# A two-layer graph and attention kernel: one load queue, a second expert's products in the first attention's last pairs, rows of the graph layer placed under the experts, and an end of the second attention written out by hand

## The chip, the cores and the metric

The kernel runs on one core of a Trainium2 chip. The metric is the device time of one execution in microseconds. Five engines run their own instruction queues: TensorE (PE, with its weight loads listed apart as PEld), VectorE (DVE), ScalarE (ACT), GpSimd (POOL) and SyncE (SP), which issues nearly all DMA transfers. Matmuls of float32 data appear in the trace as two matmul instructions each, called halves below.

## The reference

N is 1250 nodes with 512 features, 41,250 directed edges. Cut to what matters:

```python
x = x + gnn0(layernorm(x))        # alpha = h@wc ; mean over neighbours of h@wn ; + bias
x = x + ffn0(layernorm(x))        # causal attention, 8 heads of 64, then 8 experts:
    # y = attention(...) @ Wo ; gate = softmax(y @ gate_W + gate_b)
    # hid = gelu(y @ W1[e] + b1[e]) (512 -> 256) ; out = sum_e gate_e * (hid @ W2[e] + b2[e])
x = x + gnn1(layernorm(x))        # h@W_self + mean over neighbours @ W_neigh + bias, layernorm, gamma, beta
x = x + ffn1(layernorm(x))        # depthwise conv of width 3, then attention that keeps the
    # 16 best keys of each query: softmax over those, weighted values, @ wo + wo_b
```

## The kernel before

Rows are cut into T = 10 tiles of P = 125 nodes. `tile_usual` does all the work; at its end it reads one flag, `bad`, and only if that is set runs `tile_general`, which does not happen on these inputs. The stages by the trace: edge counts and the first graph layer up to about 310 us (with the projections of the first attention), the first attention to 620, eight experts to 889, the second graph layer with convolution and projections to 1126, the second attention to 1558.

**Start.** The edge lists `dst_i` and `src_i` (125 rows each) are loaded on SP's queue, and the first node weights `w_n` (1 MB) on ScalarE's queue at the same time; on SP the first part of `X`, `w_c`, and the other four parts of `X` follow. VectorE builds one-hot matrices from the edge lists (`one_hots`), TensorE counts with them (`counts`), and node work (`node_stats` to `node_own`) is put between the rounds.

**First attention.** Its order is written out by hand. A step n is a pair of heads of one row tile, 40 steps in the tile order 7, 9, 8, 6, 5, ..., 0, and two drain steps 40 and 41. Step n makes the scores of n+1, the maxima (`largest0`) and Exp (`weights0`) of n, the transpositions of n−1 (`turns0`), the weighted values of n−2 (`values0`) and one projected quarter (`project0`). The scores of one step in small tiles share one PSUM tile `S` of 1536 columns, of which the last 512 are free. In steps 26, 29, 32 and 35 (`FILL`) TensorE also makes products of expert 0's first weights with row tiles 4 to 9 into those free columns, four matmuls spread over the step; VectorE copies the sum to `parts`, places in the memory of V that are not needed any more.

**Experts.** For each expert e, `hidden` makes the products of `yT` with W1 in three chunks of tiles (0 to 4, 4 to 8, 8 to 10) and two halves f of 128, ScalarE applies Gelu, and `outputs` multiplies with W2, while VectorE adds gate times product to X (L1320). For expert 0 the chunks from tile 4 on are taken from `parts`. Expert weights come in three places of `wpool`, two experts ahead, on SP.

**Second graph layer.** Rows (`bias1`, `gamma`, `beta1`, `v_b`, `wo_b`) and work tiles (`work1`) are opened after the experts have closed their places, and the rows loaded there. For each tile: a norm of X (`stats`, `normed`), transpositions (L859), ScalarE's copy to `inT`, the product with `w_m` (L865). The scheduler, not the hand, orders this part and most of the experts.

**Second attention.** Again by hand, 40 steps (i, j) of a row tile and a head pair. Per step and head: best 8, replaced, next 8 (VectorE), Exp and Sign (ScalarE), product of the two `e·sg` (GpSimd, L1636), transpositions in five groups (`turn1`, `keep1`, one PSUM bank), values of the step n−2, and the sums of the softmax (`sums1`, `sums_exp1`, `sums_over1`, `sums_wide1`, `sums_turn1`, `sums_keep1`, `scale1`). The same loop runs three steps more to drain, with conditions (`final`) for the last tile; `project1` multiplies a tile's result with `w_o`, and `finish1` adds X and stores. After the loop a count of the signs (whether each row kept exactly 16) is summed over the partitions on GpSimd with `partition_all_reduce` (L1822) and gives `bad`.

Of the kernel before, what the change touches and what calls it, by code (L numbers as in the profile page):

```python
# [9 lines left out]
F32 = mybir.dt.float32  # L10
# [10 lines left out]
P = 125  # L21
# [551 lines left out]
def tile_usual(ctx: ExitStack, tc: tile.TileContext, a: dict, out: bass.AP):  # L573
# [24 lines left out]
    def span(t0, t1):  # L598
        return slice(t0 * P, t1 * P)

    def load_w(w, name, queue=nc.sync):
        t = wpool.tile([128, K, D], F32, tag="w", name=name)
        queue.dma_start(t, w.rearrange("(k p) f -> p k f", p=128))
        return t

    def load_expert(e):
# [53 lines left out]
    nc.sync.dma_start(dst_i, a["dst_c"])  # L660
    nc.sync.dma_start(src_i, a["src_c"])

    w_n = load_w(a["wn"], "w_n", nc.scalar)
    for t in range(0, T, 2):
        nc.sync.dma_start(X[:, t : t + 2, :], a["x"].rearrange("(t p) d -> p t d", p=P)[:, t : t + 2, :])
        if t == 0:
            w_c = load_w(a["wc"], "w_c")

    bias0 = row(a["bias0"], "bias0")
# [321 lines left out]
    def on(n):  # L991
        return 0 <= n < len(steps)
# [17 lines left out]


    SMALL = 6 * K
    FILL = {26: (0, 8, 10), 29: (1, 8, 10), 32: (0, 4, 8), 35: (1, 4, 8)}
    ps_s0a_pool = tc.tile_pool(name="ps_s0a", bufs=1, space=PSUM, side="right", reuse_waits="tile")
    ps_s0 = {0: ps_s0a_pool.__enter__()}
    shared = [None]
# [60 lines left out]
    parts = [V_all[:, 4 * D + f * 6 * P : 4 * D + (f + 1) * 6 * P] for f in range(2)]  # L1077

    def part(f, t0, t1):
        return parts[f][:, span(t0 - 4, t1 - 4)]  # L1080

    with tc.tile_pool(name="att0", bufs=2, side="right", reuse_waits="tile") as at0:
# [60 lines left out]
        def fills0(n):  # L1145

            if n not in FILL:
                return []
            f, t0, t1 = FILL[n]
            w1 = experts[0][0]  # L1150
            ps = shared[0][:, 1024 : 1024 + (t1 - t0) * P]

            def fill(k):
                nc.tensor.matmul(ps, w1[:, k, f * 128 : (f + 1) * 128], yT[:, k, span(t0, t1)],
                                 start=(k == 0), stop=(k == K - 1))
                if k == K - 1:
                    nc.vector.tensor_copy(part(f, t0, t1), ps)

            return [lambda k=k: fill(k) for k in range(K)]

# [58 lines left out]
        for n in range(len(steps) + 2):  # L1219
            finish0()  # L1220
            turns = turns0(n - 1)
            fills = fills0(n)

            def turn(last=False):
                for f in turns if last else turns[:1]:
                    f()
                del turns[: len(turns) if last else 1]
                for f in fills if last else fills[:1]:
                    f()
                del fills[: len(fills) if last else 1]  # L1230

            if n > 0:
                largest0(n, 0)
            turn()
            values0(n - 2, 0)
            if n > 0:
                weights0(n, 0)
            largest0(n, 1)
            if len(turns) > 2:
                turn()  # L1240
            values0(n - 2, 1)
            scores0(n + 1, 0)
            weights0(n, 1)
            if len(turns) > 3:
                turn()
            values0(n - 2, 2)
            sums_over0(n)
            scale0(n - 2)
            if len(turns) > 1:
                turn()  # L1250
            scores0(n + 1, 1)
            if len(turns) > 1:
                turn()
            turn(last=True)
# [17 lines left out]
    close(ps_s0a_pool)  # L1272
    psum_pool = tc.tile_pool(name="psum_moe", bufs=3, space=PSUM, reuse_waits="tile")
    psum = psum_o = psum_pool.__enter__()


    with tc.tile_pool(name="moe", bufs=2, side="right") as moe:
# [45 lines left out]
        for e in range(E):  # L1323
# [8 lines left out]
            late = CHUNKS[1:] + CHUNKS[:1] if e == 0 else CHUNKS  # L1332
            for f in range(FF // 128):
                for t0, t1 in late:
                    if e == 0 and t0 > 0:
                        nc.scalar.activation(hid[:, f, span(t0, t1)], part(f, t0, t1),
                                             AF.Gelu_apprx_tanh, bias=b1[:, f : f + 1])
                        continue
                    hidden(e, hid, w1, f, t0, t1)
            if e == 0:  # L1340
# [12 lines left out]
    rows1_pool, rows1 = pool("rows1", 1)  # L1353
    bias1 = row(a["bias1"], "bias1", pool=rows1)
    gamma = row(a["gamma"], "gamma", pool=rows1)
    beta1 = row(a["beta"], "beta1", pool=rows1)
    v_b = row(a["v_b"], "v_b", pool=rows1)
    wo_b = row(a["wo_b"], "wo_b", pool=rows1)
    slots_pool, slots = pool("slots", 1)
    work_pool, work = pool("work1", 2)  # L1360
# [146 lines left out]
    normed1(T - 1)  # L1507
    project1_(0, 2, w_k, 0)
    turn1_(T - 1)
    close(work_pool)  # L1510
    project1_(0, 2, w_k, 1, 2, 3)
    values1_(0, 2)
    for f in range(K):
# [13 lines left out]
    close(slots_pool, rows1_pool, wpool_pool, rows_pool)  # L1527
    psum_pool.__exit__(None, None, None)


# [11 lines left out]
    with (  # L1542
# [86 lines left out]
        def select1(n, a_):  # L1629
            if not 0 <= n <= last:  # L1630
                return
            sg = at1.tile([P, N], F16, tag=f"sg{a_}", name="sg", bufs=1)
            nc.scalar.activation(sg, score.pop((n, a_))[:, :N], AF.Sign, bias=found.pop((n, a_)),  # L1633
                                 accum_out=signs[:, 2 * n + a_ : 2 * n + a_ + 1])
            e = es[n, a_]
            nc.gpsimd.tensor_mul(e, e, sg)  # L1636

        def turn1(n, g):
            if not 0 <= n <= last:
# [74 lines left out]
        def project1(i, c, width=D // K):  # L1714

            y = ps_o1.tile([128, 512], F32, tag="o", name="O")[:P, :width]
            cols = slice(c * width, (c + 1) * width)
            for k in range(K):
                nc.tensor.matmul(y, oTs[i][:, k, :], w_o[:, k, cols], start=(k == 0), stop=(k == K - 1))  # L1719
# [17 lines left out]
        def keep_late1():  # L1737
            if lates:
                t, ps = lates.pop(0)
                nc.vector.tensor_add(V[:, t, :], ps[:P], v_b)  # L1740

        stacks, sums, oTs, ys, projected, lates = {}, {}, {}, {}, [], []
        with tc.manual_schedule():
            nc.sync.dma_start(w_v, a["qkv"][:, 2 * D :].rearrange("(k p) f -> p k f", p=128))
# [1 line left out]
            for a_ in range(2):  # L1746
                halves1(0, a_)
            scores1(0, 0, 2, 0, 1)
            for n in range(len(steps) + 3):


                i, c = n // K - 1, n % K
                i = i if i < T else None
                final = i == T - 1
                if i is not None and i >= 0 and c == 1 and not final:
                    sums_over1(i)
                first1(n, 0)
                values1(n - 2, 0, 5)
# [15 lines left out]
                keep1(n - 1, 1)  # L1774
                second1(n, 0)
                outputs1(n - 2)
                if i is not None and i >= 0:
                    if c == 0:
                        sums1(i)
                    if c == 1 and not final:  # L1780
                        sums_wide1(i)
                    if c == (1 if final else 2):
                        sums_turn1(i)
                        sums_keep1(i)
                    if c == (1 if final else 3):
# [4 lines left out]
                if final:  # L1790
                    project1(*((i - 1, c, D // 2) if c < 2 else (i, 0, D)))
                elif i is not None and i >= 1:
                    project1(i - 1, c)
                scores1(n + 1, 0, 2)
                keep1(n - 1, 2)
                if i is not None and i >= 0 and c == 0:
                    sums_exp1(i)
                    if final:
                        sums_over1(i)
                        sums_wide1(i)  # L1800
                if n == 0:
                    keep_late1()
                without1(n, 1)
# [10 lines left out]
                    keep_late1()  # L1814
                finish1()

        nc.vector.tensor_scalar(signs, signs, float(N - 2 * TOPK), None, op0=ALU.add)
        nc.vector.tensor_mul(signs, signs, signs)
        worst = at1.tile([P, 2], F32, name="worst", bufs=1)
        nc.vector.tensor_reduce(worst[:, 0:1], signs, AX.X, ALU.add)  # L1820
        nc.vector.tensor_copy(worst[:, 1:2], edges)
        nc.gpsimd.partition_all_reduce(worst, worst, P, bass_isa.ReduceOp.add)  # L1822
        missing = at1.tile([1, 1], F32, name="missing", bufs=1)
        nc.vector.tensor_scalar(missing, worst[0:1, 1:2], -1.0, float(NE), op0=ALU.mult, op1=ALU.add)
        nc.vector.tensor_tensor(missing, missing, worst[0:1, 0:1], ALU.max)
        nc.vector.tensor_scalar(bad, missing, 0.5, None, op0=ALU.is_gt)
# [62 lines left out]
```

## Time and profile before

| what | us |
|---|---|
| median of 3 runs | 1566.55 (1565.73 to 1567.2) |
| the profiled execution | 1567.34 |
| its span in the profile | 1565.5 |
| busy: TensorE | 1448.4 (93%) |
| busy: VectorE | 891.0 (57%) |
| busy: ScalarE | 708.6 (45%) |
| busy: GpSimd | 441.5 (28%) |

The profile is of one execution; its own time stands 1.8 us above its span. A timeline row has the start in us, the duration in us, engine, line of the kernel, operation, output and inputs, and in brackets how long the engine stood idle before it and what ended that. A window row has the stretch, its length, the busy time of each engine with the number of instructions, the granted clock of TensorE, the share of the DMA engines and GB/s.

### The profile page before, as it was taken

Reading aid. Unit: us, or ns where it says so; the run is one execution under the profiler, and the core shown is the slowest. Engines: PE = TensorE matmul, PEld = TensorE weight load, DVE = VectorE, ACT = ScalarE, POOL = GpSimd, SP = SyncE. Lnnn points to the kernel's source line nnn. Section 1 sums busy time; section 2 is a strip of 40 time slices with the busy share of each in tenths; the row PEclk is TensorE's granted clock in tenths of the full one; section 3 lists DMA queues with packets and bytes.
Section 4 is the critical chain, followed back from the end, with each engine's and each line's share of the span. In section 5 each row is a group of like instructions: output and inputs, shape, how many; then the busy total and the mean of one; then the engine's idle time right before and its main releaser. Section 6 shows DMA issues by size and latency. Waiting matters only on the chain. (4 is left out here: it accounts for less than half of the span.)

```text
span 1565.5 us, 21452 instructions
## 1 busy us (share of the span) xinstructions
PE 1448.4 (93%) x8133; PEld 949.0 (61%) x8133; DVE 891.0 (57%) x1395; ACT 708.6 (45%) x1352; POOL 441.5 (28%) x634
## 2 busy tenths in 40 slices
PE   5999999979999998999999899989898999999995
PEld 3556744457777766454444446654466777777773
DVE  7895667544444332412222434654498999999892
ACT  2334434455555543110001123331278888888882
POOL 1010000011111220000000032240177888888882
PEclk9999999989999997999999999999999999999998
DMA  4001000010101010000001100000200000000000
GB/s 146 18 0 54 1 1 0 7 44 14 41 18 48 22 26 31 27 27 27 27 27 54 47 22 19 2 26 0 80 11 11 17 19 21 21 21 21 21 8 23
DMA packets 42323, 41.12 MB, mean 26 GB/s; under 512 B 25738, under 2 KB 30084, under 8 KB 42211
## 3 DMA queue, kind: packets, MB, share of 16 engines
q1 hardware_dynamic: 41683, 38.61, 8.2%
q8 instruction: 66, 1.08, 0.3%
q10 hardware_dynamic: 528, 1.05, 0.2%
q14 instruction: 46, 0.38, 0.1%
HBM read 26.81 MB, written 2.56 MB: 19 GB/s over the span
## 5 line engine op out<-in xcount | busy, mean ns | idle before, releaser
L1636 POOL TENSOR_TENSOR e<-e,sg 125x1250 f32<-125x1250 f32 x80 | 206.1, 2577 | 36.2 <-ACT sg L1633 32.6
L1320 DVE SCALAR_TENSOR_TENSOR X<-ps_o,gate,X 125x512 f32<-125x512 f32 x80 | 60.1, 751 | 192.5 <-PE ps_o L1318 192.5
L1584 PE MATMUL S<-K,stacks 128*125 128x512 f32 (+1 forms) x480 | 124.4, 383 | 27.2 <-ACT sg L1633 23.9
L1646 PE MATMUL ps_t<-ident,e 125*125 125x125 f32 x800 | 133.8, 290 | 12.3 <-ACT R L1687 6.0
L1318 PE MATMUL ps_o<-we,hid 128*125 128x512 f32 x320 | 141.0, 595 | 0.0
L1653 ACT ACTIVATE pT<-ps_t 125x500 f32<-125x500 f32 x200 | 118.0, 590 | 49.0 <-PE ps_t L1646 48.0
L1598 DVE MAX8 best<-S 125x8 f32<-125x1250 f32 x80 | 117.0, 1462 | 36.5 <-PE S L1584 35.6
L1646 PEld LDWEIGHTS ps_t<-ident,e 125*125 125x125 f32 x800 | 106.8, 189 | 47.8 <-ACT pT L1653 27.8
L1310 PE MATMUL ps_mm<-yT,we 128*128 128x500 f32 (+1 forms) x352 | 125.9, 516 | 0.0
L1313 ACT ACTIVATE hid<-ps_mm,b 128x500 f32<-128x500 f32 (+1 forms) x44 | 26.9, 612 | 218.5 <-PE ps_mm L1310 218.5
L1618 DVE MAX8 best<-rest 125x8 f32<-125x1250 f32 x80 | 117.1, 1464 | 2.7
L1609 DVE MATCH_REPLACE8 rest<-best,S 125x1250 f32<-125x1250 f32 x80 | 116.0, 1450 | 0.0
L1702 PE MATMUL O<-pT,yT 125*64 125x125 f32 x1600 | 112.8, 279 | 0.0
L1633 ACT ACTIVATE sg<-S,below 125x1250 f16<-125x1250 f32 x80 | 104.8, 1310 | 16.4 <-POOL below L1619 16.3
L1626 ACT ACTIVATE e<-S,nm 125x1250 f32<-125x1250 f32 x80 | 104.2, 1302 | 2.7 <-DVE rest L1609 1.6
L1584 PEld LDWEIGHTS S<-K,stacks 128*125 128x125 f32 x480 | 75.4, 190 | 48.7 <-ACT sg L1633 30.3
L1318 PEld LDWEIGHTS ps_o<-we,hid 128*125 128x125 f32 x320 | 59.2, 187 | 71.6 <-issue 71.3
L1310 PEld LDWEIGHTS ps_mm<-yT,we 128*128 128x128 f32 x352 | 66.3, 189 | 59.6 <-issue 57.5
L1374 POOL TENSOR_TENSOR X<-X,beta 125x512 f32<-125x512 f32 x10 | 12.8, 1305 | 309.1 <-DMA beta<-in_beta 298.8
L1005 POOL TENSOR_TENSOR stacks<-yT,stacks 64x125 fp32r<-64x125 f32 x80 | 34.3, 428 | 232.2 <-ACT stacks L1004 228.8
L1126 ACT COPY pT<-ps_t 125x500 f32<-125x500 f32 (+3 forms) x112 | 54.8, 489 | 94.9 <-PE ps_t L1121 93.9
L1702 PEld LDWEIGHTS O<-pT,yT 125*64 125x64 f32 x1600 | 84.9, 137 | 14.2 <-issue 0.4
(230 smaller groups left out, 2668.6 us busy)
## 6 DMA issues: line engine op xcount, KB each, us to landing
we<-in_W SPq DMA_DIRECT2D x16, 512.0 KB
stacks<-stacks SPq DMA_DIRECT2D x160, 31.2 KB
stacks<-stacks SPq DMA_DIRECT2D x40, 125.0 KB
X<-in_x SPq DMA_DIRECT2D x5, 500.0 KB
out<-y SPq DMA_DIRECT2D x10, 250.0 KB
w_n<-in_wn ACTq DMA_DIRECT2D x1, 1024.0 KB
w_c<-in_wc SPq DMA_DIRECT2D x1, 1024.0 KB
w_q<-in_Wq SPq DMA_DIRECT2D x1, 1024.0 KB
```

What stands on the lines that cost most here:

```text
L1310: nc.tensor.matmul(ps[:, :n], w1[:, k, f * 128 : (f + 1) * 128], yT[:, k, span(t0, t1)], start=(k == 0), stop=(k == K - 1))
L1318: nc.tensor.matmul(ps[:P], hid[:, f, span(t, t + 1)], w2[:, f, :], start=(f == 0), stop=(f == FF // 128 - 1))
L1584: nc.tensor.matmul(score[n, a_][:, n0:n1], stacks[i][:, x, h, :], K2[:, h, n0:n1], start=(x == 0), stop=(x == 1))
L1598: nc.vector.max(out=top[:, 0:8], in_=score[n, a_][:, :N])
L1609: nc.vector.match_replace(out=rest, in_to_replace=top[:, 0:8], in_values=score[n, a_][:, :N], imm_value=LOWEST)
L1618: nc.vector.max(out=top[:, 8:16], in_=rest)
L1626: nc.scalar.activation(e, score[n, a_][:, :N], AF.Exp, bias=found[n, a_][0])
L1633: nc.scalar.activation(sg, score.pop((n, a_))[:, :N], AF.Sign, bias=found.pop((n, a_)), accum_out=signs[:, 2 * n + a_ : 2 * n + a_ + 1])
L1636: nc.gpsimd.tensor_mul(e, e, sg)
L1646: nc.tensor.transpose(turned[n, g][:P, span(b - g0, b - g0 + 1)], es[n, b // T][:, span(b % T, b % T + 1)], ident[:P, :P])
L1653: nc.scalar.activation(pTs[n][:, g0:g1, :], turned.pop((n, g))[:P, : (g1 - g0) * P].rearrange("p (t n) -> p t n", n=P), AF.Relu)
L1702: nc.tensor.matmul(outs[n][a_ * DH : (a_ + 1) * DH, :P], V[:, t, h * DH : (h + 1) * DH], pT[:, a_ * T + t, :], start=(t == 0), stop=(t == ...
```

## The change

- `w_n` is loaded on SP's queue like the others, behind the edge lists and the first part of X.
- `FILL` gets four more entries: expert 1's products for tiles 4 to 9, in steps 37, 38 and in the drain steps 40 and 41 (which take a PSUM tile of their own). From step 37 on two of the four matmuls of a fill have places of their own. Expert 1 takes its chunks from tile 4 on from `parts`, and V's pool is closed after expert 1 instead of after expert 0.
- The pools of the graph layer's rows and work tiles are opened, and the rows loaded, before the experts' pool; `gate` and `stacks` stay open to the end of the layer.
- The loop of the second attention runs over the 40 steps alone, and what followed is written out: all of tile 8's projection in one PSUM tile, the last sums earlier, tile 9's projection one term at a time. The last `e·sg` goes to VectorE. The check sums go through a matmul with ones instead of GpSimd's reduction.

```diff
-    w_n = load_w(a["wn"], "w_n", nc.scalar)
     for t in range(0, T, 2):
         nc.sync.dma_start(X[:, t : t + 2, :], ...)
         if t == 0:
+            w_n = load_w(a["wn"], "w_n")
             w_c = load_w(a["wc"], "w_c")
...
-    FILL = {26: (0, 8, 10), 29: (1, 8, 10), 32: (0, 4, 8), 35: (1, 4, 8)}
+    FILL = {26: (0, 0, 8, 10), 29: (0, 1, 8, 10), 32: (0, 0, 4, 8), 35: (0, 1, 4, 8),
+            37: (1, 0, 8, 10), 38: (1, 0, 4, 8), 40: (1, 1, 8, 10), 41: (1, 1, 4, 8)}
...
-            f, t0, t1 = FILL[n]
-            w1 = experts[0][0]
+            e, f, t0, t1 = FILL[n]
+            w1 = experts[e][0]
+            if not on(n):
+                shared[0] = ps_s0[n % 2].tile([128, 3 * 512], F32, name="S")
             ps = shared[0][:, 1024 : 1024 + (t1 - t0) * P]
...
             values0(n - 2, 0)
+            for f in fills[:1] if n > 36 else ():
+                fills.pop(0)()
             if n > 0:
                 weights0(n, 0)
...
             if len(turns) > 3:
                 turn()
+            for f in fills[:1] if n > 36 else ():
+                fills.pop(0)()
             values0(n - 2, 2)
...
+    rows1_pool, rows1 = pool("rows1", 1)
+    bias1 = row(a["bias1"], "bias1", pool=rows1)
+    gamma = row(a["gamma"], "gamma", pool=rows1)
+    beta1 = row(a["beta"], "beta1", pool=rows1)
+    v_b = row(a["v_b"], "v_b", pool=rows1)
+    wo_b = row(a["wo_b"], "wo_b", pool=rows1)
+    work_pool, work = pool("work1", 2)
     with tc.tile_pool(name="moe", bufs=2, side="right") as moe:
...
-                    if e == 0 and t0 > 0:
+                    if e < 2 and t0 > 0:
-                        nc.scalar.activation(hid[:, f, span(t0, t1)], part(f, t0, t1), ...
+                        nc.scalar.activation(hid[:, f, span(t0, t1)], part(e, f, t0, t1), ...
...
+            if e == 1:
                 close(qkv0_pool)
-    close(gate_pool, stacks_pool)
...
-            nc.gpsimd.tensor_mul(e, e, sg)
+            (nc.vector if 2 * n + a_ == 2 * last + 1 else nc.gpsimd).tensor_mul(e, e, sg)
...
+        def signs_over1():
...
+            ps = ps_o1.tile([128, 512], F32, tag="o", name="ps_w1")[:1, :2]
+            nc.tensor.matmul(ps, ones, worst, start=True, stop=True)
...
-            for n in range(len(steps) + 3):
+            for n in range(len(steps)):
...
-        nc.gpsimd.partition_all_reduce(worst, worst, P, bass_isa.ReduceOp.add)
...
+            n, i = len(steps), T - 1
+            sums1(i)
+            values1(n - 2, 0, 5)
+            select1(n - 1, 1)
+            turn1(n - 1, 0)
+            values1(n - 2, 5, 8)
+            keep1(n - 1, 0)
+            sums_exp1(i)
+            turn1(n - 1, 1)
+            values1(n - 2, 8, T)
+            keep1(n - 1, 1)
+            outputs1(n - 2)
+            sums_over1(i)
+            sums_wide1(i)
+            y0 = ps_s1a.tile([P, 3 * 512], F32, name="S")
+            y1 = ps_s1b.tile([P, 3 * 512], F32, name="S")
+            project1(i - 1, 0, D, y0[:, :D])
+            turn1(n - 1, 2)
+            keep1(n - 1, 2)
+            finish1()
+            sums_turn1(i)
+            sums_keep1(i)
+            turn1(n - 1, 3)
+            keep1(n - 1, 3)
+            R = sums.pop(i)
+            oT = oTs[i]
+            nc.vector.tensor_mul(oT[:, : K - 1, :], oT[:, : K - 1, :], R[:, : K - 1, :])
+            def terms(*ks):
+                for k in ks:
+                    nc.tensor.matmul(y1[:, :D], oT[:, k, :], w_o[:, k, :], start=(k == 0), stop=(k == K - 1))
+            terms(0)
+            turn1(n - 1, 4)
+            signs_over1()
+            terms(1)
+            keep1(n - 1, 4)
+            values1(n - 1, 0, T)
+            terms(2)
+            nc.vector.tensor_mul(oT[:, K - 1, :], outs.pop(n - 1)[:, :P], R[:, K - 1, :])
+            terms(K - 1)
+            projected.append((i, slice(0, D), y1[:, :D]))
+            finish1()
```

More of the change, by code (lines that the diff above doesn't have):

```diff
@@ L599, in span, with load_w @@
         return slice(t0 * P, t1 * P)
-    def load_w(w, name, queue=nc.sync):
+    def load_w(w, name):
         t = wpool.tile([128, K, D], F32, tag="w", name=name)
-        queue.dma_start(t, w.rearrange("(k p) f -> p k f", p=128))
+        nc.sync.dma_start(t, w.rearrange("(k p) f -> p k f", p=128))
         return t
@@ L1076, in tile_usual, with part @@
     b2_h = gate_p.tile([4 * E, D], F32R, name="b2_h")
-    parts = [V_all[:, 4 * D + f * 6 * P : 4 * D + (f + 1) * 6 * P] for f in range(2)]
-    def part(f, t0, t1):
-        return parts[f][:, span(t0 - 4, t1 - 4)]
+    parts = [V_all[:, 4 * D + f * 6 * P : 4 * D + (f + 1) * 6 * P] for f in range(4)]
+    def part(e, f, t0, t1):
+        return parts[2 * e + f][:, span(t0 - 4, t1 - 4)]
     with tc.tile_pool(name="att0", bufs=2, side="right", reuse_waits="tile") as at0:
@@ L1156, in fill @@
                 if k == K - 1:
-                    nc.vector.tensor_copy(part(f, t0, t1), ps)
+                    nc.vector.tensor_copy(part(e, f, t0, t1), ps)
             return [lambda k=k: fill(k) for k in range(K)]
@@ L1334, in tile_usual @@
                 for t0, t1 in late:
-                    if e == 0 and t0 > 0:
-                        nc.scalar.activation(hid[:, f, span(t0, t1)], part(f, t0, t1),
-                                             AF.Gelu_apprx_tanh, bias=b1[:, f : f + 1])
+                    if e < 2 and t0 > 0:
+                        nc.scalar.activation(hid[:, f, span(t0, t1)], part(e, f, t0, t1), AF.Gelu_apprx_tanh,
+                                             bias=b1[:, 2 * e + f : 2 * e + f + 1])
                         continue
@@ L1348, in tile_usual @@
                 manual.__exit__(None, None, None)
+            if e == 1:
                 close(qkv0_pool)
-    close(gate_pool, stacks_pool)
[L1353 to L1358, printed above, removed]
     slots_pool, slots = pool("slots", 1)
-    work_pool, work = pool("work1", 2)
     g1_pool, g1 = pool("g1", 1, "left")
@@ L1509, in tile_usual @@
     turn1_(T - 1)
-    close(work_pool)
     project1_(0, 2, w_k, 1, 2, 3)
@@ L1526, in tile_usual @@
     manual.__exit__(None, None, None)
-    close(slots_pool, rows1_pool, wpool_pool, rows_pool)
+    close(slots_pool, work_pool, rows1_pool, gate_pool, stacks_pool, wpool_pool, rows_pool)
     psum_pool.__exit__(None, None, None)
@@ L1712, in outputs1, with project1 @@
             nc.scalar.copy(oTs[i][:, j, :], outs.pop(n)[:, :P])
-        def project1(i, c, width=D // K):
-            y = ps_o1.tile([128, 512], F32, tag="o", name="O")[:P, :width]
+        def project1(i, c, width=D // K, y=None):
+            if y is None:
+                y = ps_o1.tile([128, 512], F32, tag="o", name="O")[:P, :width]
             cols = slice(c * width, (c + 1) * width)
@@ L1740, in keep_late1 @@
                 nc.vector.tensor_add(V[:, t, :], ps[:P], v_b)
+        def signs_over1():
+            nc.vector.tensor_scalar(signs, signs, float(N - 2 * TOPK), None, op0=ALU.add)
+            nc.vector.tensor_mul(signs, signs, signs)
+            worst = at1.tile([P, 2], F32, name="worst", bufs=1)
+            nc.vector.tensor_reduce(worst[:, 0:1], signs, AX.X, ALU.add)
+            nc.vector.tensor_copy(worst[:, 1:2], edges)
+            ps = ps_o1.tile([128, 512], F32, tag="o", name="ps_w1")[:1, :2]
+            nc.tensor.matmul(ps, ones, worst, start=True, stop=True)
+            missing = at1.tile([1, 2], F32, name="missing", bufs=1)
+            nc.vector.tensor_copy(missing, ps)
+            nc.vector.tensor_scalar(missing[:, 1:2], missing[:, 1:2], -1.0, float(NE), op0=ALU.mult, op1=ALU.add)
+            nc.vector.tensor_tensor(missing[:, 0:1], missing[:, 0:1], missing[:, 1:2], ALU.max)
+            nc.vector.tensor_scalar(bad, missing[:, 0:1], 0.5, None, op0=ALU.is_gt)
         stacks, sums, oTs, ys, projected, lates = {}, {}, {}, {}, [], []
@@ L1748, in tile_usual @@
             scores1(0, 0, 2, 0, 1)
-            for n in range(len(steps) + 3):
+            for n in range(len(steps)):
                 i, c = n // K - 1, n % K
-                i = i if i < T else None
-                final = i == T - 1
-                if i is not None and i >= 0 and c == 1 and not final:
+                if i >= 0 and c == 1:
                     sums_over1(i)
@@ L1776, in tile_usual @@
                 outputs1(n - 2)
-                if i is not None and i >= 0:
+                if i >= 0:
                     if c == 0:
                         sums1(i)
-                    if c == 1 and not final:
+                    if c == 1:
                         sums_wide1(i)
-                    if c == (1 if final else 2):
+                    if c == 2:
                         sums_turn1(i)
                         sums_keep1(i)
-                    if c == (1 if final else 3):
+                    if c == 3:
                         scale1(i)
@@ L1789, in tile_usual @@
                 turn1(n - 1, 2)
-                if final:
-                    project1(*((i - 1, c, D // 2) if c < 2 else (i, 0, D)))
-                elif i is not None and i >= 1:
+                if i >= 1:
                     project1(i - 1, c)
@@ L1795, in tile_usual @@
                 keep1(n - 1, 2)
-                if i is not None and i >= 0 and c == 0:
+                if i >= 0 and c == 0:
                     sums_exp1(i)
-                    if final:
-                        sums_over1(i)
-                        sums_wide1(i)
                 if n == 0:
@@ L1815, in tile_usual @@
                 finish1()
[L1817 to L1826, printed above, removed]
+            n, i = len(steps), T - 1
[39 more added lines that the diff above has]
+            finish1()
     anew = nc.values_load(bad[0:1, 0:1], min_val=0, max_val=1)
```

## The prediction

> **What bounds the kernel now.** I read the 40 slices first. TensorE is near full in almost all of them; the exceptions that the change touches are the first slice, the last, and the 16th (587 to 626 us), with busy 8 and clock 7. Line 1 is TensorE's busy share in tenths, line 2 its granted clock.
>
> ```profile
> PE   5999999979999998999999899989898999999995
> PEclk9999999989999997999999999999999999999998
> ```
>
> The fourth place that it touches is the border from the experts to the second graph layer. I therefore read the timeline at each border, and windows by step of the first attention.
>
> At the start nothing can run before the two edge lists land:
>
> ```profile
> 0.72 0.42 ACTq L603 DMA_DIRECT2D w_n<-in_wn  x1
> 5.91 0.33 DVE L724 CAST dst_f<-dst_i 125x330 f32<-125x330 int32 x1 [4.80 <-DMA dst_i<-in_dst_c]
> 9.55 0.33 DVE L725 CAST src_f<-src_i 125x330 f32<-125x330 int32 x1 [3.30 <-DMA src_i<-in_src_c]
> ```
>
> VectorE then works 9.90 of 10 us (10 to 20 us) and 8.9 to 9.8 of 10 up to 60 us, so what it starts earlier ends earlier.
>
> Steps of the first attention by window (length, then PE, PEld, DVE, ACT, POOL busy, clock, DMA share, GB/s): pair 34 without fills, 35 with fills, 38, 39, and the projections before the experts.
>
> ```profile
> 575.20:579.30 4.10, 3.78 (x30) 2.86 (x30) 1.48 (x6) 2.50 (x9) 0.70 (x2) 1.00 0.13 33
> 579.30:586.50 7.20, 6.71 (x37) 4.03 (x36) 2.06 (x6) 2.50 (x9) 1.61 (x4) 1.00 0.14 34
> 594.85:599.35 4.50, 3.69 (x23) 3.11 (x23) 1.22 (x6) 1.54 (x7) 0.30 (x1) 0.79 0.00 0
> 599.35:603.83 4.48, 3.84 (x16) 2.75 (x16) 1.15 (x5) 1.60 (x7) 0.30 (x1) 0.50 0.00 0
> 612.64:620.41 7.77, 7.00 (x40) 6.81 (x39) 1.04 (x5) 0.00 (x0) 0.00 (x0) 0.66 0.03 7
> ```
>
> The clock halves at about 597 us: little matmul work is left per step. At the border to the graph layer TensorE waits for norms that start only after the last expert's output:
>
> ```profile
> 889.52 0.75 DVE L1320 SCALAR_TENSOR_TENSOR X<-ps_o,gate,X 125x512 f32<-125x512 f32 x1 [0.96 <-PE ps_o L1318]
> 893.71 1.30 PE L859 MATMUL ps_tp<-ident,h 125*128 125x125 f32 x8 [4.22 <-DVE h L644]
> 895.04 8.49 PE L865 MATMUL ps_mm<-w_m,slot 128*125 128x512 f32 x16
> ```
>
> At the end two waits of GpSimd for nothing the profile names ("issue") stand in the chain:
>
> ```profile
> 1532.70 2.57 POOL L1636 TENSOR_TENSOR e<-e,sg 125x1250 f32<-125x1250 f32 x1 [1.54 <-ACT sg L1633]
> 1541.37 0.41 POOL L1822 PARTITION_ALL_REDUCE worst<-worst  x1 [5.73 <-issue]
> 1541.65 0.68 POOL L1676 COPY rb<-r 125x512 f32<-125x512 f32 x1
> 1549.34 1.23 POOL L1690 TENSOR_TENSOR oT<-oT,R 128x500 f32<-128x500 f32 x1 [7.00 <-issue]
> 1550.62 6.65 PE L1719 MATMUL O<-w_o,oT 128*125 128x512 f32 x8 [5.86 <-POOLq L568]
> 1557.31 0.69 DVE L1727 TENSOR_TENSOR y<-X,O 125x512 f32<-125x512 f32 x1 [12.08 <-PE O L1719]
> ```
>
> **1. One load queue.** Transfers of 125 rows run at a steady 123 GB/s with a DMA share of 0.33 (windows 10 to 34 us, when only X moves), about 5 of 16 engines. Each edge list (161.1 KB) is thus 1.34 us. Data begin at about 1.8 us. With w_n sharing those engines half and half, dst ends at 1.8+2×1.34 = 4.5 and is used at 5.91: 1.4 us from last byte to use. With w_n behind, src ends at 1.8+2×1.34 = 4.5 and is used at 5.9 instead of 9.55: 3.6 us. The first X part (4.2 us) and then w_n's share on these engines (2.7) end at 11.4, usable at 12.8; w_n's first reader is TensorE at 26.8, or 23.2 when moved. So w_n's later place costs nothing; if that slack of 10 us were gone, each us would stall the node products and the counts behind them. Bounds 0 and 4.3. Taken: **3.6**.
>
> **2. Second expert's products in pairs 37, 38 and drain steps 40, 41.** Removed from the experts, where TensorE never idles: 16 matmul halves of 500 columns at 0.42 us and 16 of 250 at 0.21 (L1310, start to start): 10.1 us. Added in the steps: the same. In pair 35 fills of 8×0.42 = 3.36 us lengthened the step by 7.20−4.10 = 3.10, so 92% lies on the path: +9.3. Waits are added too: in pairs 37 and 38 the scores' Exp now waits for the second fill (same PSUM tile) and the third fill for the second head's Exp; queued behind that fill are the values, the next scores and the projection. Exp and maximum rows of 0.37 and 0.29 with 0.2 to 0.6 between suggest +0.8 in all (bounds 0 and 2). The four copies to V (0.68 for 500 columns) run beside the projection.
>
> Against that stands the clock. If these products keep TensorE busy enough for the full clock, the old work from 597 us on runs at its earlier price: four projections 2.07→1.16 (3.6 us), three sets of transposition and values 1.13→0.73 (1.2), gate products 1.69→0.94 (0.7), the 24 last matmuls 4.80→3.15 (1.7): −7.2. Sum: −10.1+9.3+0.8−7.2 = **−7.2**. If the clock falls all the same in step 39, which has no fill, fills of steps 40 and 41 cost up to double until it recovers: +5, net −2. Bounds −10 and +2.
>
> [...]
>
> The later closing of V's pool puts two casts of the adjacency behind four Gelus (0.5 to 0.7 each) on ScalarE, which is 2.3 of 20 us busy there: nothing. Expert 1's first output waits for the last Gelu (0.68), covered by its first product (0.86).
>
> **3. Places under the experts'.** With rows and work tiles of their own, the built order puts four tiles' statistics and two norms between the last expert's output additions. Transpositions can follow the last output at 889.3 and the first product 1.33 later (893.71 to 895.04), at 890.6 instead of 895.04: 4.4 us. The cold start goes: 16 halves took 8.49, the next 16 take 7.13: 1.4. VectorE has 0.97 us free per output tile; statistics need about 1.2, and one burst (reciprocal, wait for ScalarE's root, two norms, statistics: 2.3) exceeds gap plus spare PSUM bank by 0.6. Sum **5.2** (bounds 3 and 6). The five row loads move ahead of the third expert's weights on SP: 5×250 KB at 123 GB/s is 10.4 us, plus 4 for the weights, from 619: landed by about 634, read at about 675. Nothing; rival 4 prices the cover gone.
>
> **4. End by hand.** The last e·sg on VectorE: additions there cost 0.27 (128 columns) and 0.69 (512), so 1250 give 1.5 instead of 2.57. Worth nothing: tile 8's whole projection now stands before the group that needs it and covers it; without that, 1.1. TensorE's queue from 1534.4: this projection 3.6 (L800's price), three transposition groups with copies (next weights, sums, next) at 1.4 each, ending 1541.6; one term of the last projection 0.86, last group 0.7, a term 0.86, 40 value matmuls 2.4, two terms 1.7: 1548.1. The sums' copy (0.68) follows VectorE's reciprocal at 1534.7, five us ahead of its reader. The check sums (four VectorE operations, about 0.9, then a 1×2 matmul) fit before their place. The addition takes 0.2+0.7: 1549.0 against 1558.00. Output store and branch (7.5) stay. **9.0** (bounds 5, if the clock halves on the way, and 10).
>
> **Sum.** 3.6+7.2+5.2+9.0 = 25.0. The profiled execution took 1567.34 (span 1565.5 and 1.8 around it), 0.8 above the median: 1542.3 there, **1541.5** against the median 1566.55.
>
> **Rivals.**
> 1. The clock halves in the pairs all the same: +5, 1546.5. For it: step 39 has about the same matmul share as the stretch before 597. Against: fills on both sides.
> 2. The start gains nothing since the edge lists are bound elsewhere: 1545.1. [...]
> 3. GpSimd's 5.7 us before the sums' copy stays without the reduction: copy done at 1542.3 instead of 1535.4, sums' group 2.9 later: 1544.4. Against: no such gap elsewhere on that line.
> 4. Slower: the row loads stand in SP's one queue before the third expert's weights and need memory of the first attention. Every us by which it comes free after 660 stalls TensorE; beyond 685 the gain is gone, at 690 the time is 1571. Against: the attention's tiles are last read at 605 to 613.
> 5. Everything better: fills partly hidden, no VectorE burst: −4, 1537.5.
>
> **How the numbers follow.** Forecast 0.50, rivals 0.23, 0.07, 0.05, 0.03, 0.12. Range 1535.5 to 1550: rivals 1 to 3 or two of them together (1550), rival 5 with the upper bounds of parts 1 and 4 (about 1535.5). 0.2% is 3 us, about what a measurement here can tell; all but rival 4 are far beyond it: faster 0.96, same 0.01, slower 0.03.
>
> **What would show it.** Right: src_f near 6 us; clock 1.00 in steps 39 to 41; experts' first product near 620 less 3.6 and less 0 to 4; expert 1's block 10 shorter; no wait above 1.5 us between L1318's heir and the first w_m product; no "issue" waits on GpSimd at the end, and 14 to 16 us from the last sign to the last addition. Wrong: DMA waits at the experts, clock 0.5 in the drain steps, TensorE waiting for the sums.

## The result, and the profile after

The changed kernel takes 1542.82 us (median of 4 runs, 1540.8 to 1544.26) against 1566.14 for the kernel before on the same chip: a ratio of 0.9849, 95% interval 0.9832 to 0.9866. That is 23.3 us less; the forecast was 1541.5 in a range of 1535.5 to 1550. Run again on another occasion it took 1543.74 (ratio 0.9863, 0.9847 to 0.9878). The profiled execution took 1544.26 (span 1542.5), so 23.1 less than the profiled 1567.34.

Between marks that both traces have, in us:

| from one mark to the next | before | after | difference | in the working |
|---|---|---|---|---|
| start to the cast of src_f | 9.55 | 6.12 | −3.4 | −3.6 |
| to the experts' first product | 610.89 | 613.16 | +2.3 | +2.9 |
| to the last expert's last addition to X | 269.08 | 259.23 | −9.9 | −10.1 |
| to the second tile's product with w_m | 15.17 | 9.34 | −5.8 | −5.2 |
| to the second attention's last Sign | 626.53 | 629.51 | **+3.0** | 0 |
| to the last addition to y | 26.09 | 16.89 | −9.2 | −9.0 |

In the 40 slices of the profile after, the first line is TensorE's busy share in tenths and the second its granted clock. The 7 in the 16th slice and the 8 in the last are gone from the clock:

```profile
PE   6999999979999998999999999989988999999997
...
PEclk9999999989999999999999999999999999999999
```

The timeline of VectorE at the start. Both edge lists come earlier, the second by 3.43 us:

```profile
4.30 0.33 DVE L724 CAST dst_f<-dst_i 125x330 f32<-125x330 int32 x1 [3.20 <-DMA dst_i<-in_dst_c]
6.12 0.33 DVE L725 CAST src_f<-src_i 125x330 f32<-125x330 int32 x1 [1.48 <-DMA src_i<-in_src_c]
```

Windows from projection to projection at the end of the first attention (length; busy time of PE, PEld, DVE, ACT, POOL; clock; DMA share; GB/s). The first two hold the products of pairs 37 and 38, the fourth and fifth are lengthened by those of steps 40 and 41, the last ends at the experts' first product:

```profile
585.77:592.03 6.26, 5.18 (x35) 3.71 (x35) 1.22 (x5) 2.53 (x10) 1.24 (x4) 1.00 0.08 20
592.03:600.70 8.67, 7.05 (x39) 4.39 (x39) 1.72 (x7) 1.74 (x8) 0.30 (x1) 1.00 0.00 0
600.70:604.16 3.46, 2.12 (x17) 1.49 (x15) 1.83 (x6) 1.50 (x7) 0.13 (x1) 1.00 0.02 5
604.16:607.99 3.83, 3.83 (x24) 2.65 (x24) 0.58 (x2) 0.80 (x3) 0.16 (x1) 1.00 0.00 0
607.99:613.01 5.02, 5.02 (x22) 2.66 (x22) 0.99 (x3) 0.27 (x1) 0.00 (x0) 1.00 0.00 0
613.01:619.28 6.27, 5.50 (x49) 5.31 (x49) 1.72 (x6) 0.00 (x0) 0.00 (x0) 1.00 0.31 96
```

They sum to 33.51 against 3.77+4.42+4.48+4.28+4.32+9.87 = 31.14 between the same projections of the trace before. The clock is 1.00 in all of them, where it had been 0.5 from 597 to 618 us.

The border to the graph layer in the timeline after. The transpositions (L859) begin before the last addition to X, and no wait for `h` stands ahead of them:

```profile
878.31 1.02 PE L859 MATMUL ps_tp<-ident,h 125*128 125x125 f32 x8
...
878.51 0.75 DVE L1336 SCALAR_TENSOR_TENSOR X<-ps_o,gate,X 125x512 f32<-125x512 f32 x1 [0.96 <-PE ps_o L1334]
...
879.57 7.13 PE L865 MATMUL ps_mm<-w_m,slot 128*125 128x512 f32 x16 [0.24 <-ACT slot L1384]
```

The end, from the timelines of VectorE, TensorE and GpSimd. The copy to `rb` waits for VectorE's reciprocal alone, and no "issue" wait is left on GpSimd:

```profile
1518.80 1.46 DVE L1644 TENSOR_TENSOR e<-e,sg 125x1250 f32<-125x1250 f32 x1 [2.71 <-ACT sg L1641]
...
1520.50 3.70 PE L1728 MATMUL S<-w_o,oT 128*125 128x512 f32 x8
...
1520.76 0.61 POOL L1684 COPY rb<-r 125x512 f32<-125x512 f32 x1 [3.08 <-DVE r L1678]
...
1532.23 1.98 PE L1866 MATMUL S<-w_o,oT 128*125 128x512 f32 x4
...
1534.25 0.69 DVE L1736 TENSOR_TENSOR y<-X,S 125x512 f32<-125x512 f32 x1 [1.61 <-PE S L1866]
```

**Where the 3.0 us went.** The tile loop of the graph layer keeps the lead (16.8 us throughout). Some 1.7 go in the 24 key products behind tile 9's transposition, which take 6.92 instead of 5.23 us, and the other 1.3 early in the second attention. First the line of these products before, then, from the trace after, their line and the two windows of 3.41 us around its start:

```profile
1039.83 5.23 PE L1453 MATMUL ps_mm<-yT,w_k 128*128 128x250 f32 x24
...
1023.03 6.92 PE L1462 MATMUL ps_mm<-yT,w_k 128*128 128x250 f32 x24
...
1020.55:1023.96 3.41, 1.41 (x9) 1.32 (x10) 2.57 (x4) 1.46 (x4) 3.41 (x4) 1.00 0.00 0
1023.96:1027.37 3.41, 3.41 (x10) 2.77 (x9) 0.75 (x4) 1.36 (x5) 3.41 (x4) 0.50 0.00 0
```

A stretch in which TensorE is idle for 2.00 us (most of a wait of 2.54 us for tile 9's normed row) is followed by one at half clock. In both whole traces, up to the last product, half clock comes only in whole stretches of 3.41 us, and the starts of all of them lie whole multiples of 3.413 us apart (after: 20.45, then 88 to 90 and 290, 294, 320, 326, 335, 338 stretches later). Without the stretches that begin behind the last product, before had 61.4 us of half clock, after 34.1.

### The profile page after: what moved, and what is told of

Same layout as the page of the kernel before. It is cut to its first block, busy times and chain, and to the rows that moved or that the text cites. A ratio compares the mean times of both kernels' runs of the same rounds, so it can differ in the third digit from the quotient of the medians.

```text
span 1542.5 us, 21431 instructions
## 1 busy us (share of the span) xinstructions
PE 1438.5 (93%) x8127; PEld 939.2 (61%) x8127; DVE 894.3 (58%) x1402; ACT 708.0 (46%) x1351; POOL 438.0 (28%) x631
## 4 chain that ended last, share of the span: by engine, by line
PE 70%; DVE 13%; ACT 11%; issue 3%; POOL 2%; DMA 0%; ACTq 0%; SPq 0%; DVEq 0%; POOLq 0%
PE ps_o L1334 9%; PE ps_mm L1326 7%; PE S L1592 5%; PE ps_mm L865 5%; PE ps_t L1654 5%; PE ps_mm L800 4%; PE ps_mm L1462 4%; PE S L1034 4%; PE ps_o L870 4%; PE ps_t L1122 4%; PE O L1143 3%; PE O L1710 3%; ACT sg L1641 3%; PE bank L768 2%; PE O L1187 2%
## 5 line engine op out<-in xcount | busy, mean ns | idle before, releaser
L1326 PE MATMUL ps_mm<-yT,we 128*128 128x500 f32 (+1 forms) x320 | 115.8, 520 | 0.0
L1326 PEld LDWEIGHTS ps_mm<-yT,we 128*128 128x128 f32 x320 | 60.3, 189 | 55.2 <-issue 53.3
```

The lines of the kernel that those rows point to most:

```text
L1326: nc.tensor.matmul(ps[:, :n], w1[:, k, f * 128 : (f + 1) * 128], yT[:, k, span(t0, t1)], start=(k == 0), stop=(k == K - 1))
```

## The experiments

**The changed kernel again, three parts undone.** The first run is the yardstick.

> The changed kernel unaltered, as the yardstick of this set. In its first profile the half clock of TensorE came only in whole stretches of 3.41 us that lie on one grid of 3.41 us, and two of them (1023.96 and 1133.19 us) hit work that ran at full clock before the change; that gave back 1.7 + 1.3 = 3.0 us. Theory A: the grid's position against the work is an accident of each execution; then this profile shows the half stretches elsewhere by up to 3.41 us, the 24 key products after L1462's transposition take anything from 5.2 to 6.9 us, and times spread over 1540.5 to 1544.5. Theory B: the grid starts with the program; then the half stretches lie at 1010.3, 1024.0, 1112.7, 1133.2, 1163.9 and 1174.2 again, within 0.2 us, in the same work.

1543.74 us. The stretches lie at 1009.7, 1023.4, 1112.1, 1173.6 and 1183.8 us: 0.6 us off the first profile's grid, none at 1133, and one new at 603.53. The 24 key products took 6.72. So theory A holds for the grid, but the loss of 1.7 us is not a rare one: of the nine profiles in which this place has the changed kernel's order, eight show 6.6 to 6.9 us there and one 5.23 (the run below with the old end and a product with ones). In part 1 alone and part 2 alone below, as before, it is 5.23. The whole interval in which the 3.0 us were lost, from the second tile's product to the last Sign, lies in these nine profiles between 0.9 us below and 3.1 above the 626.5 of before, so the size of that loss changes from one execution or variant to the next.

```diff
+    w_n = load_w(a["wn"], "w_n", nc.scalar)      # ahead of X
-            w_n = load_w(a["wn"], "w_n")
```

> The changed kernel with w_n back on ScalarE's queue, ahead of X. Theory (w_n shares the engines that carry the edge lists): dst_f near 5.9 and src_f near 9.5 us instead of 4.3 and 6.1, every later row of the start 3.4 us later, time +3.4 against the changed kernel: 1546 (with the clock grid's accidents 1544.5 to 1548). Rival (the edge lists are bound by something else): src_f stays near 6.1 and the time at 1542.8. Second rival: the 3.4 us are lost again before the experts' first product, time +0 to +1 although src_f is late.

1547.63, ratio to before 0.9890 (0.9875 to 0.9905), 3.9 above the yardstick. dst_f 6.20, src_f 9.74, as the theory said. (The profiled run is the fastest of the four, 1542.05 at a clock of 0.992; the other three took 1547.5 to 1547.9 at 0.988.)

```diff
-            37: (1, 0, 8, 10), 38: (1, 0, 4, 8), 40: (1, 1, 8, 10), 41: (1, 1, 4, 8)}
-                    if e < 2 and t0 > 0:
+                    if e == 0 and t0 > 0:
```

> The changed kernel without the four new entries of the table FILL; the second expert's first products are made in the experts again. Theory (two thirds of the gain are the clock): experts +9.9, the steps from pair 37 to the last projection shorter by only 2.4, because the clock is 0.5 for five or six stretches of 3.41 us from about 594 us: time +7.5, 1550.3. Rival (the clock would stay full here without the products, the half stretches of before were an accident of the grid): the steps shorter by 2.4 + 7.2 = 9.6, experts +9.9: time +0.3, 1543. Rival (products hide wholly under other engines' work): steps unchanged, +9.9: 1552.7.

1541.57 (4 runs, 1540.81 to 1546.45; ratio 0.9861): no loss at all, against my theory and as the first rival said. In the profile the clock is full in every step; the last addition to X comes at 878.95 against 879.09 in the yardstick, so experts and steps cancel. The same six intervals sum to 24.10 here. That splits the +2.4 of the comparison: 33.51−24.10 = 9.4 for the products at equal clock, 31.14−24.10 = 7.0 for the clock. But did the products bring the clock, or would it have been full anyway? Four runs could not tell; the next two sets do.

```diff
-    rows1_pool, rows1 = pool("rows1", 1)         # and its five rows, and work1: behind the experts again
+    close(gate_pool, stacks_pool)
+    rows1_pool, rows1 = pool("rows1", 1)
```

> The changed kernel with the second graph layer's rows and work tiles opened after the experts again (row loads too). Theory: the transpositions of the first tile wait some 4.2 us for its normed row after the last expert's output, the clock is 0.5 for one stretch over the first w_m products (8.5 instead of 7.1 us): +5.8, 1548.6. Rival (the cold clock is an accident of the grid and not of the wait): +4.4, 1547.2, w_m's first 16 halves 7.1. Rival (the wait moves to another tile's norms, the order of VectorE being as long): +1 or less.

1547.32, ratio 0.9893 (0.9877 to 0.9908), 3.6 above the yardstick by the medians and 0.0030 by the ratios (4.7 us). Its timeline has the wait back:

```profile
884.40 1.81 PE L859 MATMUL ps_tp<-ident,h 125*128 125x125 f32 x8 [4.22 <-DVE h L644]
886.09 8.03 PE L865 MATMUL ps_mm<-w_m,slot 128*125 128x512 f32 x16
...
895.27 7.13 PE L865 MATMUL ps_mm<-w_m,slot 128*125 128x512 f32 x16 [0.30 <-ACT slot L1386]
```

From the last addition (880.22) to the second tile's product it is 15.05 us against 9.34: 5.7 in that stretch, as the theory said. That the medians show less may be the clock elsewhere (single runs at 0.985 to 0.990); this was not separated.

**Parts alone, the old end, a better border.**

```diff
-    w_n = load_w(a["wn"], "w_n", nc.scalar)
+            w_n = load_w(a["wn"], "w_n")         # behind X's first part; all else as before
```

> The kernel before with part 1 alone: w_n on the one load queue behind X's first part. Every step of the first attention then comes 3.5 us earlier, which is one clock stretch of 3.41 us and 0.1 us. Theory A (the fall of the clock at 597 us hangs on where the grid's stretches lie in the steps, and a few tenths of a us decide): the fall comes in some executions and not in others, mean clocks of single runs in two groups some 0.006 apart, time 1562 with the fall and 1555 without. Theory B (the fall comes with these steps whenever the second expert's products are not in them; that it stayed away in e2 was a rare accident): clock 0.979 to 0.981 in nearly all runs, 3.5 below before: 1561. Theory C (the shift alone took the fall away): no run with the fall, 10 below before, 1554.

1562.31 (12 runs) against 1565.89: ratio 0.9973 (0.9962 to 0.9985), −3.6. Mean clocks: four runs at 0.983 to 0.984 (1558.6 to 1560.1), eight at 0.977 to 0.981 (1561.0 to 1564.5). In its profile the fall lasts two stretches (from 603.32), where before it lasted six. This lies between theories A and B: as I read the clocks, the fall comes in most runs and its length varies with the grid, but one profile alone shows it.

```diff
+            37: (1, 0, 8, 10), 38: (1, 0, 4, 8), 40: (1, 1, 8, 10), 41: (1, 1, 4, 8)}
+                    if e < 2 and t0 > 0:         # with the new places and positions of the products; all else as before
```

> The kernel before with part 2 alone: the four new entries of FILL (and V's place closed after the second expert). The prediction's working: clock full from 597 us on, experts -9.9, steps +2.4: 7.2 to 7.5 below before (1557). Theory A: the same here, since the products make the stretches full wherever the grid lies; clock up by 0.006. Rival (the full clock in the changed kernel came from the shift and not from the products): clock stays 0.980 and the steps grow by 9.4 at least, up to 15 with half clock: time 0 to +5 against before.

1557.69 (6 runs) against 1565.89: ratio 0.9949 (0.9931 to 0.9966), −8.2. Mean clock 0.984 to 0.987, up by 0.006 in the mean, and no half clock between 333 and 885 us in the profile. So the products do bring the full clock, without the shift.

```diff
-            for n in range(len(steps)):          # then the end by hand
+            for n in range(len(steps) + 3):      # and partition_all_reduce, e*sg on GpSimd
```

> The changed kernel with the end of the second attention as before: the loop runs three steps further, the last product with the signs on GpSimd, the check sums by GpSimd's all-reduce. Theory (9.2 measured between the last Sign and the last y addition): two waits of GpSimd of 5.7 and 7.0 us for nothing that the profile shows come back, last Sign to last addition 26 us instead of 17, time +9.2: 1552.5. Rival (part of the 9.2 is the half clock over the last eight matmuls, an accident of the grid): +6 to +7, with L1719's heir at 4.0 to 4.5 us for eight instead of 6.65.

1552.69, ratio 0.9915 (0.9901 to 0.993), 9.5 above the changed kernel's 1543.2 (mean of its 8 runs). From the last Sign (1515.99) to the addition (1542.25) it is 26.3 us again. TensorE and GpSimd:

```profile
1526.41 0.41 POOL L1846 PARTITION_ALL_REDUCE worst<-worst  x1 [6.01 <-issue]
1526.70 0.68 POOL L1684 COPY rb<-r 125x512 f32<-125x512 f32 x1
1534.38 1.23 POOL L1698 TENSOR_TENSOR oT<-oT,R 128x500 f32<-128x500 f32 x1 [7.01 <-issue]
...
1535.67 6.54 PE L1728 MATMUL O<-w_o,oT 128*125 128x512 f32 x8 [5.86 <-POOLq L568]
```

The rival is wrong in that the slow last product is no accident: in all four profiles with this end (before, the two parts alone, e4) two stretches of half clock lie over it, behind 5.9 to 6.0 us in which TensorE is idle.

```diff
+    project1_(0, 2, w_q, 0, 1)
     turn1_(T - 2)
-    project1_(0, 2, w_q, 0, 1)
...
-    project1_(0, 2, w_k, 0)
+    project1_(0, 2, w_k, 0, 1, 2, 3)
     turn1_(T - 1)
-    project1_(0, 2, w_k, 1, 2, 3)
```

> The changed kernel with one thing more: at the border to the second attention two query products of the first two tiles stand ahead of tile 8's transposition, and all four key products ahead of tile 9's, so that TensorE has work in the two waits of 4.09 and 2.54 us for normed rows. Theory: both waits shrink to under 1.7 and 0.5, no stretch of half clock at 1010 and 1024 us (1.3 and 1.7 us): -2.4 -2.0 -2 = -6 at most, 1537. Rival (the tiles' positional sums behind these transpositions, or VectorE's copies of the key products, are what comes last): the waits move a few us on, 0 to -2.

1539.49 (5 runs), ratio to before 0.9832 (0.9817 to 0.9846): 3.7 below the changed kernel, the fastest version here, though not the 6 of the theory. The first wait shrank from 4.09 to 0.73 us. The second only changed its place: VectorE copies the query products out of PSUM, and the copies stand behind two positional sums (1.70 and 1.62 us):

```profile
1009.15 0.65 PE L859 MATMUL ps_tp<-ident,h 125*128 125x125 f32 x4 [0.73 <-DVE h L644]
...
1013.75 1.85 PE L1462 MATMUL ps_mm<-yT,w_k 128*128 128x250 f32 x8
1017.76 7.01 PE L1462 MATMUL ps_mm<-yT,w_k 128*128 128x250 f32 x24 [2.16 <-DVE qT L1465]
```

**The disputed clock, and the end taken apart.** First the kernel of e2 once more, unchanged.

> The kernel of e2 once more (no products of the second expert in the first attention's steps), for what four runs could not tell: how often the clock falls in its steps. Theory A (the fall is the rule without the products: nearly all runs of the kernel before and most of part 1 alone had it, mean clock 0.979 to 0.981, and part 2 alone took it away): most runs here have mean clock 0.982 to 0.986 and the median is 1548 to 1550, some 5 to 7 above the changed kernel; e2's first four runs were the rare ones. Theory B (with the other parts the fall is rare): clock 0.989 to 0.991 again, median 1541 to 1543, the products are worth nothing on top of the other parts.

1548.7 (4 runs, 1548.2 to 1553.31; ratio 0.9898, 0.9881 to 0.9916), as theory A said, but on another chip, where the kernel before took 2.1 us more (1566.03 against 1563.92); that the chip has a part in it is not ruled out. In the profile the clock falls at 594.08 for six stretches. The same steps in the two profiles of this one kernel, first e2, then again, in stretches of the grid:

```profile
590.08:593.50 3.42, 3.01 (x27) 2.43 (x25) 0.87 (x5) 1.31 (x7) 0.00 (x0) 1.00 0.00 0
593.50:596.91 3.41, 2.23 (x15) 1.59 (x15) 1.12 (x5) 1.38 (x8) 0.29 (x1) 1.00 0.00 0
596.91:600.33 3.42, 2.23 (x15) 1.59 (x15) 0.90 (x4) 1.10 (x6) 0.29 (x1) 1.00 0.00 0
```

```profile
590.66:594.08 3.42, 2.62 (x24) 2.03 (x22) 1.22 (x6) 1.54 (x7) 0.18 (x1) 1.00 0.00 0
594.08:597.49 3.41, 3.15 (x14) 2.42 (x14) 0.77 (x3) 0.72 (x3) 0.12 (x1) 0.50 0.00 0
```

The work stands almost alike (the projection ahead of drain step 40 starts at 593.90 and 594.04), the grid 0.58 us apart. A stretch that lies just between two projections, 2.62 of 3.42 us busy, brought the fall; stretches only 2.23 busy that hold a whole projection (593.90, 597.47) did not. (In part 1 alone one did: 2.00 busy, with the projection of 600.14 in it.)

```diff
 FILL = {26: (0, 0, 8, 10), ..., 35: (0, 1, 4, 8)}   # f1 without the four new entries
```

> f1 without the products of the second expert in the first attention's steps: the same question with the other order at the border, so with the later half stretches elsewhere. Theory A: 5 to 7 above f1, 1545, mean clock lower by 0.004 to 0.006. Theory B: within 1.5 of f1 (1538 to 1541), clock the same.

1547.18 (4 runs), ratio 0.9883 (0.9869 to 0.9897), 7.7 above f1; clock 0.982 to 0.983 against 0.988 to 0.992; the fall at 593.65 for six stretches. That is theory A.

```diff
-        nc.gpsimd.partition_all_reduce(worst, worst, P, bass_isa.ReduceOp.add)   # in e4
+            nc.tensor.matmul(ps, ones, worst, start=True, stop=True)
```

> e4 (the old end) with one thing taken away: the check sums are reduced over partitions by a product with ones and not by GpSimd's all-reduce. Theory (GpSimd's two unnamed waits of 6.0 and 7.0 us belong to the all-reduce, which stands between its ordinary operations): rb copied 5 us earlier and the last multiplication of oT right after the sums' group, at about 1529 instead of 1534.4; 5 to 8 us below e4, 1545 to 1548. Rival 3 of the prediction (the waits belong to this copy and this multiplication): both waits stay, 1552. What is left above the changed kernel, 2 to 5 us, is then the order by hand.

1544.43, ratio 0.9863 (0.9846 to 0.9879): 8.3 below e4. Both "issue" waits are gone (the lines of GpSimd, then the last product):

```profile
1518.81 0.61 POOL L1684 COPY rb<-r 125x512 f32<-125x512 f32 x1 [1.62 <-DVE r L1678]
1524.48 1.24 POOL L1698 TENSOR_TENSOR oT<-oT,R 128x500 f32<-128x500 f32 x1 [5.06 <-ACT R L1695]
...
1526.17 3.67 PE L1728 MATMUL O<-w_o,oT 128*125 128x512 f32 x8 [0.61 <-DVE y L1736]
```

From the last Sign (1512.78) to the addition (1529.88) it is 17.1 us, against 16.9 by hand. What the hand order adds is that the check sums are done ahead of the last product: from the end of the addition to the end of the span it is 7.5 us by hand and 8.8 here.

```diff
-            (nc.vector if 2 * n + a_ == 2 * last + 1 else nc.gpsimd).tensor_mul(e, e, sg)
+            nc.gpsimd.tensor_mul(e, e, sg)
```

> The changed kernel with the last e*sg on GpSimd again (2.57 instead of 1.46 us). The prediction's working: worth nothing, since tile 8's projection (3.6 us) covers it: within 1 of the changed kernel, 1543, last Sign to last addition 15.7 us as before. Rival (it starts later too, behind what is queued on GpSimd, and the transposition groups behind the projection come up to 1.1 us later): +1.1, 16.8 us.

1543.21, and 16.9 us from the last Sign (1517.52) to the addition (1534.42): worth nothing, as worked out. The 15.7 us "as before" of the expectation was a misreading: the changed kernel has 16.9 too, so the rival's 1.1 us did not come either.

## Why the prediction was right, step by step

**One load queue: right.** 3.4 in the trace, −3.6 alone, +3.9 when undone, against 3.6. With two issuers src_f came at 9.55 (before) and 9.74 us (undone in the changed kernel) instead of 6.12 and 6.39 (the changed kernel's two profiles), so rival 2 is wrong.

**Second expert's products: right in its terms, and right about the cause.** Experts 9.9 (10.1 worked out); products with their waits on the path 9.4 (9.3+0.8); the clock 7.0 in the same steps (7.2). Alone the part is worth 8.2, on top of f1 7.7, and e2's two sets, taken as one, have a median of 1547.3, some 4 above the changed kernel. Without the clock it is worth nothing (878.95 against 879.09). No long wait of TensorE stands ahead of the fall at 597.45 us in the trace before: between 588 and 600 us the longest is 0.47 us. What the working lacked is that the fall is a matter of tenths of a us: with the grids 0.58 us apart it came in the second profile of e2's kernel and stayed away in the first. Rival 1, the clock falling in the pairs all the same, shows only as one stretch near 603 in a0, e3, e4 and f1, four of the nine profiles with the products.

**Places under the experts': right, 5.8 in the trace against 5.2** (the gap from the last addition to the first product 5.5 to 1.06, the cold start 1.4), 5.7 when undone. The 0.6 for VectorE's burst did not appear, as rival 5 had it. The row loads cost nothing; nothing waits for them at the experts (rival 4).

**End by hand: right in size, 9.2 against 9.0, but the working followed TensorE's queue and did not say which edit wins it.** One of them, the reduction without GpSimd, gives 8.3 of the 9.5. The chain: the all-reduce has unnamed waits of 6.0 before and 7.0 us behind it; the multiplication behind it is late; TensorE stands idle 5.9 us; its last eight products then run at half clock, 6.54 instead of 3.67. Rival 3, which left the waits with the copy, is wrong. What fills the 6.01 and the 7.01 us no run shows; with a product with ones in place of the reduction both are gone (e5).

**What failed: the term that was not there.** The sum counted the lead as kept from 905 us to the end. In the profile it lost 3.0 in half-clock stretches that hit new work. By the sum of the terms as measured (3.4−2.3+9.9+5.8+9.2 = 26.0) the profiled execution would have taken 1541.3; it took 1544.26. That the forecast of 1541.5 is only 1.3 off is partly luck: the terms came out 1.0 better than worked out, which made up for a part of the loss that the sum left out.

Two of the prediction's signs did not come, and both contradict its own sum. It looked for the experts' first product near 620 less 3.6 and less 0 to 4, while its terms give 620.4−3.6+2.9 = 619.7; 619.28 came. And it looked for 14 to 16 us from the last Sign to the last addition, while 26.1−9.0 is 17.1; 16.9 came.

Across 99 timed executions of the kernels here, each about its own kernel's mean, 1 us more of half clock (twice the span times one less the mean clock) goes with 0.32 us more of time. Before has 63.1 us of it on average and after 35.1. By an estimate from these numbers about 9 of the 22 us are clock, and the rest is work and waits taken off the path. That agrees with the pieces: 7.0+1.4+2.9−3.0 = 8.3.

## What to carry to other kernels

Fill a thin stretch of TensorE's path with work that is due later anyway: even when none of it is hidden, it can pay by the clock of everything around it (part 2 alone: 8.2 us, mean clock 0.980 to 0.986). Look for a lone custom operation on GpSimd between its ordinary ones near the end, for its waits (here 6.0 and 7.0 us) have no name in the profile. Before a comparison of a few us, look at the mean granted clock of every run: two sets of four runs of one kernel, on two chips, differed by 7.1 us here, of which the kernel before showed 2.1.

## What was not expected of the hardware

- The half clock came in whole stretches of 3.41 us on one grid. Its place against the program's start took values all over a stretch in the 14 profiles (from 0.1 us, before, to 3.4, after), and with it which work was slow.
- A stretch in which TensorE was 2.6 of 3.4 us busy brought the half clock (before, e2 again), one 2.23 busy did not (e2), one 2.00 busy did (part 1 alone, 599.91 to 603.32). So the busy share by the profile alone is not what decides; nor does a full projection inside, for there is one in the second and in the third. What does was not settled, nor why the key products at 1023 us are hit in eight of nine profiles.
- Once halved, the clock stayed at 0.50 through stretches 3.15, 2.92, 3.09 and 2.23 us busy and through the first of two that were wholly busy (e2 again, 594.08 to 611.15 us); in a0 (603.53) it came back after one wholly busy stretch.
